# Attention probabilities turned by VectorE in 32x32 blocks instead of by TensorE, in the second batch of each middle group

## The chip, the cores and the metric

The kernel runs on one core of one Trainium2 chip. The metric is the device time of one launch in microseconds (us). The engines are named as in the profile: PE is TensorE (PEld its weight loads), DVE is VectorE, ACT is ScalarE, POOL is GpSimd, SP is SyncE, which here only issues DMAs.

## The reference, cut to what matters

Sixteen batches of 128 rows with 1024 features go through one layer: cross attention (32 query heads, 8 key and value heads, 32 features each) with a residual, and a feed-forward product with a residual, both after a layernorm.

```
B, S, EMBED, NUM_Q, NUM_KV, HEAD_DIM = 16, 128, 1024, 32, 8, 32
Q = layernorm(x) @ Wq + bq;  K = ctx @ Wk + bk;  V = ctx @ Wv + bv
scores = einsum('bhgqd,bhkd->bhgqk', Q, K) / sqrt(HEAD_DIM)
w = softmax(scores, axis=-1)
y = einsum('bhgqk,bhkd->bhgqd', w, V)
x = x + y @ Wo + bo
x = x + ffn_scale * (ei(layernorm(x)) @ ffn_kernel)      # ei: last 205 features scaled by -4
```

All is float32. On TensorE a float32 matmul is two passes, each with its own weight load, so the profile counts each matmul twice; the transposes by TensorE are one pass.

## The kernel before

The sixteen batches are taken in eight groups of two (GB = 2, T = 256 rows). While one group's attention runs, the PE works for its neighbours: the output projection of the group before (`out_proj`, names o_u, o_v, o_c), keys and values of the next (`prep_k`, `prep_v`), queries of the next (`prep_q`, names q_u, q_v, q_c), and the feed-forward products (`ffn`, name f). Groups 1 to 6 are the middle groups; the first and the last are run in their own way.

A small planner, the class `Stream`, writes all this out in one fixed order. It keeps a clock `now` by estimated PE time. `stream.add` queues work in pieces, each of which says how long it holds the PE; `stream.later(us, fn)` sets an event at a planned time; `stream.run(until)` fires events that are due and takes pieces in between. Each engine then executes its own instructions in that order, and waits where data or a buffer is not ready. There are no priorities at run time.

Attention of a group has four steps, one for each batch and half of the heads (`a` = 0 or 1, 16 query heads each), in the order batch 0, batch 1, batch 0, batch 1. In a step:

- `scores` (L568): 16 matmuls of 32 rows each; head group `i` of four uses the PE's row tile `i` and writes its own PSUM bank, tile `sc`. The four tiles come from the pool `ps_sc` with four buffers.
- For each `i`, at planned times 0.7 + 2.4 i: `exponentials` (L580 a row maximum by DVE, L584 four exponentials by ACT), and 2.3 us later `divide` (L595, L596, both DVE), which leaves the probabilities `p` with queries on the partitions.
- Half a step later, less 3 us, `turn` (L601): four transposes of 128x128 by PE into PSUM, and a copy to SBUF by ACT (L603), tile `pt`: now the keys are on the partitions.
- Near the end of the step `weighted` (L611): for each `i` one matmul of 32 columns by 512, four column tiles of the PE side by side, tile `av`; ACT copies the result to `yT` (L619), which `out_proj` reads in the next group.

The planned length of a step is `length` (23.2 us in most middle groups). The loop over steps:

```
pts = attend(b, a, length)
stream.run(start + length - 2.0)      # the last step: until the queue is empty
stream.run(stream.now, lambda: None in pts)
weighted(b, a, pts)
stream.now += 1.0
```

Weights of the projections come in pieces of 512 KB through a ring of eight buffers (`fetch`, L225), one for each that has been used; rows for the next groups, contexts and residuals are loaded from DRAM. All of these are issued by SP, in the planner's order. `through_dram` and `split_blocks` (L728) already use DVE's transposes of 32x32 blocks for the layernormed rows.

## Time and profile before

| what | value |
|---|---|
| time, three runs | median 788.25 us (787.9 to 791.28) |
| profiled execution | 788.44 us, of which the profiled span is 786.7 us |
| granted PE clock, mean | 0.997 |
| busy: PE, DVE, ACT, POOL | 767.2, 486.3, 322.4, 112.2 us |
| DMA | 192.42 MB, mean 245 GB/s; main queue 74.9% of 16 engines |

In the profile an instruction group reads: line, engine, operation, output<-input, size, number, then busy time and the mean of one in ns, then the idle time of the engine just before and what ended it. A duration of a matmul includes the pipeline behind it, so several overlap, and busy time of the PE is the union. A timeline row reads: start in us from the span's start, duration, engine, line, operation, count.

### The profile page before, as it was taken

Reading aid. Unit: us, or ns where it says so; the run is one execution under the profiler, and the core shown is the slowest. Engines: PE = TensorE matmul, PEld = TensorE weight load, DVE = VectorE, ACT = ScalarE, POOL = GpSimd, SP = SyncE. Lnnn points to the kernel's source line nnn. Section 1 sums busy time; section 2 is a strip of 40 time slices with the busy share of each in tenths; the row PEclk is TensorE's granted clock in tenths of the full one; section 3 lists DMA queues with packets and bytes.
Section 4 is the critical chain, followed back from the end, with each engine's and each line's share of the span. In section 5 each row is a group of like instructions: output and inputs, shape, how many; then the busy total and the mean of one; then the engine's idle time right before and its main releaser. Section 6 shows DMA issues by size and latency. Waiting matters only on the chain.

```text
span 786.7 us, 13740 instructions
## 1 busy us (share of the span) xinstructions
PE 767.2 (98%) x5008; PEld 571.6 (73%) x5008; DVE 486.3 (62%) x886; ACT 322.4 (41%) x1261; POOL 112.2 (14%) x142
## 2 busy tenths in 40 slices
PE   5998999999999999999999999999999999999997
PEld 4886884589746997479864898558984699556476
DVE  2158647756766567566774667856676666765552
ACT  0254764444334443344433444334434445575100
POOL 4154703020010102010020200202001010103000
PEclk9999999999999999999999999999999999999999
DMA  9999799988698776978778785987869657763802
GB/s 248 344 309 303 273 341 392 268 226 282 216 322 230 238 235 232 306 204 261 239 240 271 213 272 188 305 257 202 266 209 328 206 192 238 250 202 104 264 27 81
DMA packets 99268, 192.42 MB, mean 245 GB/s; under 512 B 8240, under 2 KB 57456, under 8 KB 99200
## 3 DMA queue, kind: packets, MB, share of 16 engines
q1 hardware_dynamic: 97568, 189.43, 74.9%
q0 software_dynamic: 528, 1.12, 0.6%
q10 hardware_dynamic: 1104, 0.98, 0.6%
q8 instruction: 40, 0.66, 0.3%
q14 instruction: 28, 0.23, 0.1%
HBM read 161.09 MB, written 30.41 MB: 243 GB/s over the span
## 4 chain that ended last, share of the span: by engine, by line
PE 88%; DVE 4%; DMA 2%; issue 2%; ACT 1%; POOL 1%; SPq 0%; POOLq 0%; DVEq 0%
PE f L323 14%; PE o_u L662 13%; PE q_u L451 12%; PE o_v L662 7%; PE tpp L601 7%; PE q_v L451 6%; PE k L323 6%; PE v L323 6%; PE sc L568 4%; PE av L611 4%; PE q L323 3%; PE o_c L662 3%; PE q_c L451 3%; DVE p L596 1%; DMA piece<-o 1%
## 5 line engine op out<-in xcount | busy, mean ns | idle before, releaser
L584 ACT ACTIVATE p<-sc,negm 128x128 f32<-128x128 f32 x512 | 181.1, 368 | 134.4 <-DVE negm L580 72.5
L603 ACT COPY pt<-tpp 128x512 f32<-128x512 f32 x128 | 74.6, 591 | 148.1 <-PE tpp L601 147.9
L580 DVE TENSOR_REDUCE negm<-sc 128x4 f32<-128x512 f32 x128 | 86.8, 680 | 59.3 <-PE sc L568 59.3
L584 ACT ACTIVATION_READ_ACCUMULATOR p<-sc,negm 128x1 f32 x512 | 105.5, 206 | 0.0
L323 PE MATMUL f<-wf_sb,x2l 128*128 128x512 f32 x256 | 104.3, 408 | 0.0
L323 PE MATMUL f<-wf_sb,x2h 128*128 128x512 f32 x256 | 100.5, 393 | 0.0
L596 DVE TENSOR_TENSOR p<-p,inv 128x512 f32<-128x512 f32 x128 | 90.9, 710 | 4.4
L451 PE MATMUL q_u<-t,piece 128*128 128x128 f32 x672 | 81.3, 275 | 0.0
L601 PEld LDWEIGHTS tpp<-ident,p 128*128 128x128 f32 x512 | 62.2, 141 | 24.9 <-issue 16.8
L601 PE MATMUL tpp<-ident,p 128*128 128x128 f32 x512 | 76.4, 274 | 3.7 <-DVE p L596 3.5
L451 PEld LDWEIGHTS q_u<-t,piece 128*128 128x128 f32 x672 | 78.0, 192 | 0.1
L180 POOL TENSOR_TENSOR x<-x,bo_b 128x256 f32<-128x256 f32 x64 | 53.6, 862 | 155.7 <-DMA x<-in_x_dram 155.7
L323 PE MATMUL v<-wv_sb,cT 128*128 128x256 f32 x256 | 62.2, 393 | 9.0 <-DMA wv_sb<-in_L_xattn_Wv_dram 7.1
L662 PE MATMUL o_v<-piece,s 128*128 128x512 f32 x128 | 60.3, 598 | 0.5 <-DVE x L676 0.5
L323 PEld LDWEIGHTS v<-wv_sb,cT 128*128 128x128 f32 x256 | 48.4, 197 | 15.8 <-DVE cT L349 9.4
L662 PE MATMUL o_u<-piece,s 128*128 128x512 f32 x128 | 59.2, 594 | 0.6 <-DVE x L676 0.6
L323 PE MATMUL k<-cT,wk_sb 128*128 128x256 f32 x256 | 58.3, 380 | 1.0 <-DVE cT L349 1.0
L662 PE MATMUL o_u<-piece,yT 128*128 128x512 f32 x128 | 58.6, 599 | 0.0
L323 PEld LDWEIGHTS f<-wf_sb,x2l 128*128 128x128 f32 x256 | 48.2, 188 | 10.6 <-issue 1.1
L323 PEld LDWEIGHTS k<-cT,wk_sb 128*128 128x128 f32 x256 | 47.9, 190 | 10.2 <-issue 2.6
L323 PEld LDWEIGHTS f<-wf_sb,x2h 128*128 128x128 f32 x256 | 48.2, 188 | 9.6 <-issue 0.5
L568 PEld LDWEIGHTS sc<-kT,qT 32*128 32x128 f32 x1024 | 31.4, 186 | 25.8 <-issue 25.8
(86 smaller groups left out, 935.1 us busy)
## 6 DMA issues: line engine op xcount, KB each, us to landing
piece<-o SPq DMA_DIRECT2D x64, 512.0 KB, 5.0
piece<-q SPq DMA_DIRECT2D x56, 512.0 KB, 5.1
piece<-in_L_xattn_Wq_dram SPq DMA_DIRECT2D x50, 512.0 KB, 5.2
piece<-in_L_xattn_Wo_dram SPq DMA_DIRECT2D x48, 512.0 KB, 4.6
xn<-in_x_dram SPq DMA_DIRECT2D x16, 512.0 KB, 6.8
x<-in_x_dram SPq DMA_DIRECT2D x16, 512.0 KB, 4.6
ctx<-in_ctx_dram SPq DMA_DIRECT2D x60, 128.0 KB, 6.6
out_dram<-x SPq DMA_DIRECT2D x15, 512.0 KB, 2.7
```

Of the source, the lines that this page charges most:

```text
L180: lambda cut=cut: nc.gpsimd.tensor_add(x_t[:, cut], x_t[:, cut], bo_b[:, cut]) and None,
L323: nc.tensor.matmul(mm, lhsT=lhsT, rhs=rhs, start=k == 0, stop=k == n - 1)
L451: nc.tensor.matmul(mm if part is None else mm[:, part], lhsT=lhsT, rhs=rhs, start=start and n == k == 0, stop=k == len(some) - 1, skip_gro ...
L568: nc.tensor.matmul(tiles[i][:, g], lhsT=qT[rows, g], rhs=kT[rows, a, cols], start=True, stop=True,)
L580: nc.vector.tensor_reduce(negm, tile_, AX.X, ALU.max, negate=True)
L584: nc.scalar.activation(p[:, g], tile_[:, g], AF.Exp, bias=negm[:, g : g + 1], accum_out=total[:, g : g + 1],)
L596: nc.vector.tensor_mul(p, p, inv.unsqueeze(2).to_broadcast([P, NG, S]))
L601: nc.tensor.transpose(tp[:, g], p[:, g], ident)
L603: nc.scalar.copy(pt, tp)
L611: nc.tensor.matmul(mm[i * HD : (i + 1) * HD], lhsT=vs[b][:, h * HD : (h + 1) * HD], rhs=pts[i], start=True, stop=True,)
L662: nc.tensor.matmul(mm, lhsT=lhsT[:, 2 * k + c], rhs=w[:, c], start=start and k == c == 0, stop=k == c == 1, skip_group_check=True,)
```

## The change

In the second batch of each middle group (`by_blocks`: batches 3, 5, 7, 9, 11, 13; 12 steps of the 32), the probabilities are no longer turned by PE.

- DVE transposes each 32x32 block of `p` in place (`turn_blocks`) after `divide`. Partition quarter `k` then holds the keys of every block `t`, for the queries of block `k`.
- `weighted_blocks` multiplies with the PE divided in 16 tiles of 32x32: for key block `t`, head group `i` and query block `k` one matmul of 32 keys by 32 features against 4 x 32 columns; the four `t` are summed in PSUM. Row tile `k` writes its own PSUM bank.
- Each quarter of the partitions needs all keys' values. So the values of such a batch are stored to DRAM, and loaded four times, once for each quarter (`load_values`), into half of the buffers `pt_all` that the other batch's turned probabilities use. This is done after each of the first batch's two sums, as these buffers are overwritten between.
- The four score tiles become one tile of four banks with one buffer, which `weighted_blocks` uses for its sums as well. Turned probabilities of the other steps go to one fixed buffer `pt_all` instead of a pool of four.
- The planned lengths are 22.4 for 23.2, and 18.6 for 19.2. The block sum stands at `length - 4.0` in its step.

```
-    ps_sc = ctx.enter_context(tc.tile_pool(name="ps_sc", bufs=4, space=PSUM))
+    ps_sc = ctx.enter_context(tc.tile_pool(name="ps_sc", bufs=1, space=PSUM))
...
             vs[b] = v
+            if by_blocks(b):
+                stream.later(2.0, lambda b=b, v=v: nc.sync.dma_start(out=v_dram[b], in_=v) and None)
...
-        tiles = [ps_sc.tile([P, NG, S], FP, tag="sc", name=f"sc_{b}_{a}_{i}") for i in range(NI)]
+        sc = ps_sc.tile([P, NI, NG, S], FP, tag="sc", name=f"sc_{b}_{a}")
...
+    NK = S // HD
+    pt_all = const.tile([P, NI, NG * S], FP, name="pt_all")
+    v_dram = [dram.tile([P, KV], FP, name=f"v_dram{b}") for b in range(B)]
...
-        pt = work.tile([P, NG, S], FP, tag="pt", name=f"pt_{b}_{a}_{i}", bufs=4)
-        nc.scalar.copy(pt, tp)
+        nc.scalar.copy(pt_all[:, i].rearrange("p (g s) -> p g s", g=NG), tp)
...
+    def by_blocks(b):
+        return GB <= b < B - GB and b % GB == 1
+
+    def repeated(b):
+        vr = pt_all[:, 2 * (b % GB) : 2 * (b % GB) + 2].rearrange("p i n -> p (i n)")
+        return vr.rearrange("p (t n) -> p t n", t=NK)
+
+    def load_values(b):
+        for k in range(NK):
+            nc.sync.dma_start(
+                out=repeated(b)[k * HD : (k + 1) * HD],
+                in_=v_dram[b].rearrange("(t r) n -> r t n", t=NK),
+            )
+
+    def turn_blocks(p):
+        blocks = p.rearrange("p g (t k) -> p g t k", t=NK)
+        nc.vector.transpose(blocks, blocks)
+
+    def weighted_blocks(b, a, pts):
+        av = ps_sc.tile([P, NK, NG, S], FP, tag="sc", name=f"av_{b}_{a}")
+        for t in range(NK):
+            for i in range(NI):
+                head = slice(i * HD, (i + 1) * HD)
+                for k in range(NK):
+                    rows = slice(k * HD, (k + 1) * HD)
+                    nc.tensor.matmul(
+                        av[head, k, :, :HD],
+                        lhsT=repeated(b)[rows, t, a * P + i * HD : a * P + (i + 1) * HD],
+                        rhs=pts[i][rows, :, t * HD : (t + 1) * HD],
+                        start=t == 0,
+                        stop=t == NK - 1,
+                    )
+        yTs[b, a] = work.tile(S4, FP, tag="yT", name=f"yT{b}_{a}", bufs=4)
+        nc.scalar.copy(
+            yTs[b, a].rearrange("p g (k q) -> p k g q", k=NK), av[:, :, :, :HD]
+        )
...
+                def by_vector():
+                    divide(b, a, i, p, total)
+                    turn_blocks(p)
+                    pts[i] = p
...
+                if by_blocks(b):
+                    stream.later(2.3, by_vector)
+                else:
+                    stream.later(2.3, lambda: divide(b, a, i, p, total))
+                    stream.later(length / 2 - 3.0, by_tensor)
...
-            length = 17.4 if first else 23.2 if grp < NGRP - 2 else 19.2
+            length = 17.4 if first else 22.4 if grp < NGRP - 2 else 18.6
...
+                if by_blocks(b):
+                    stream.run(start + length - 4.0)
+                    stream.run(stream.now, lambda: None in pts)
+                    weighted_blocks(b, a, pts)
+                    stream.now += 2.1
+                    if q == 2 * NA - 1:
+                        stream.run(start + length, lambda: stream.queue)
+                    else:
+                        stream.run(start + length)
+                    continue
...
                 weighted(b, a, pts)
                 stream.now += 1.0
+                if by_blocks(b + 1):
+                    load_values(b + 1)
```

More of the change, by code (lines that the diff above doesn't have):

```diff
@@ L568, in scores @@
                 nc.tensor.matmul(
-                    tiles[i][:, g],
-                    lhsT=qT[rows, g],
-                    rhs=kT[rows, a, cols],
-                    start=True,
-                    stop=True,
+                    sc[:, i, g], lhsT=qT[rows, g], rhs=kT[rows, a, cols], start=True, stop=True
                 )
-        return tiles
+        return sc
     def exponentials(b, a, i, tile_):
@@ L601, in turn @@
             nc.tensor.transpose(tp[:, g], p[:, g], ident)
-        pt = work.tile([P, NG, S], FP, tag="pt", name=f"pt_{b}_{a}_{i}", bufs=4)
-        nc.scalar.copy(pt, tp)
-        return pt
+        nc.scalar.copy(pt_all[:, i].rearrange("p (g s) -> p g s", g=NG), tp)
+        return True
     def weighted(b, a, pts):
@@ L613, in weighted @@
                 lhsT=vs[b][:, h * HD : (h + 1) * HD],
-                rhs=pts[i],
+                rhs=pt_all[:, i],
                 start=True,
@@ L755, in attend @@
     def attend(b, a, length):
-        tiles = scores(b, a)
+        sc = scores(b, a)
         stream.now += 1.2
@@ L763, in first, with by_tensor @@
             def first(i=i):
-                p, total = exponentials(b, a, i, tiles[i])
-                stream.later(2.3, lambda: divide(b, a, i, p, total))
-                def third():
+                p, total = exponentials(b, a, i, sc[:, i])
+                def by_vector():
+                    divide(b, a, i, p, total)
+                    turn_blocks(p)
+                    pts[i] = p
+                def by_tensor():
                     pts[i] = turn(b, a, i, p)
                     return 0.45
-                stream.later(length / 2 - 3.0, third)
+                if by_blocks(b):
[3 more added lines that the diff above has]
+                    stream.later(length / 2 - 3.0, by_tensor)
             stream.later(0.7 + 2.4 * i, first)
```

## The prediction

> **What bounds the kernel now.** I read the page's engine table first, then the chain that ended last, then the list of PE's waits.

> ```profile
> PE 767.2 (98%) x5008; PEld 571.6 (73%) x5008; DVE 486.3 (62%) x886; ACT 322.4 (41%) x1261; POOL 112.2 (14%) x142
> PE 88%; DVE 4%; DMA 2%; issue 2%; ACT 1%; POOL 1%; SPq 0%; POOLq 0%; DVEq 0%
> ```

> TensorE (PE) is busy 98% of the span and is 88% of the chain; the clock was granted whole (0.997). A microsecond taken from PE in a middle group is a microsecond of the run, as long as nothing else becomes late. PE's own waits in the list are 7.1 us on the first weights, 3.5 us on DVE's probabilities (all before 80 us), and under 2 us on anything else: nothing else is late now.

> Next, what the removed work costs. The groups:

> ```profile
> L601 PE MATMUL tpp<-ident,p 128*128 128x128 f32 x512 | 76.4, 274 | 3.7 <-DVE p L596 3.5
> L603 ACT COPY pt<-tpp 128x512 f32<-128x512 f32 x128 | 74.6, 591 | 148.1 <-PE tpp L601 147.9
> L596 DVE TENSOR_TENSOR p<-p,inv 128x512 f32<-128x512 f32 x128 | 90.9, 710 | 4.4
> L728 DVE STREAM_TRANSPOSE turn_f<-turn_f 128x512 f32<-128x512 f32 x28 | 19.7, 704 | 0.0
> ```

> Durations of matmuls overlap, so I priced by starts, in PE's timeline (start, us, count):

> ```profile
> 322.27 0.59 PE L662 MATMUL o_v<-piece,s 128*128 128x512 f32 x1
> 322.70 1.04 PE L601 MATMUL tpp<-ident,p 128*128 128x128 f32 x8
> 323.57 0.59 PE L662 MATMUL o_v<-piece,s 128*128 128x512 f32 x1
> ...
> 308.15 0.40 PE L323 MATMUL f<-wf_sb,x2h 128*128 128x512 f32 x1
> 308.48 1.07 PE L611 MATMUL av<-pt,v 128*32 128x512 f32 x8
> 309.48 1.17 PE L568 MATMUL sc<-kT,qT 32*128 32x128 f32 x32
> 310.58 0.70 PE L662 MATMUL o_u<-piece,yT 128*128 128x512 f32 x1
> ```

> Eight transposes push the stream back by 0.87 us: 0.109 each. The weighted sum (av) holds PE from 308.48 to 309.48: 1.00 us for four 32-column tiles, two passes each. The scores (sc) hold it for 1.10.

> Last, how small tiles run side by side: PE's windows of the scores alone, all from the start of the burst (busy, instructions so far):

> ```profile
> 309.47:309.68 0.21, 0.20 (x4) 1.00 0.91 371
> 309.47:309.79 0.32, 0.31 (x8) 1.00 0.94 384
> 309.47:309.90 0.43, 0.42 (x12) 1.00 0.98 400
> 309.47:310.60 1.13, 1.12 (x32) 1.00 0.96 388
> ```

> Four row tiles start together (0.007 us apart in the trace), then four more every 0.112 us; the first turn takes 0.213. Of 32 passes the last four start 0.903 after the first. All tiles that the shape allows work at once, here and in av.

> **The change part by part.** By the order of instructions it bears on 12 steps: the second batch of the six middle groups, two halves each.

> *Removed, per step.* 16 transposes by 0.109 = 1.75 us, and av 1.00: 2.75 us of PE, all on the path. ACT loses four copies of 0.59 (28 us in all): off the path, worth nothing.

> *Added on PE.* 64 matmuls of 32x32, 128 columns, two passes: 128 passes, eight for each of sixteen tiles. Borders: av stood directly before sc and shared one; the new burst stands alone, so it pays a switch out of 0.10 (o_u starts that long after sc's streams end) and 0.10 to load the next weights, beside the entry of 0.10 that av had as well. With Y for the burst and 0.1 for its end: Y + 0.30 against 2.75. Saved per step: 2.45 - Y.

> No row shows sixteen tiles. Lower bound of Y: sc's turns, eight by 0.112 = 0.90. Upper bound: only four at once as in both rows, 32 turns by 0.112 = 3.58. The rows agree in kind (every tile that exists runs), which puts Y near the lower end. But sixteen starts 0.007 apart fill a turn of 0.112 entirely, so any hiccup lengthens it. I take 1.2: saved 1.25 per step, 12 x 1.25 = 15.0 us.

> [...]

> *Added on DVE.* Four 32x32 transposes per step by 0.70 (L728's row) = 2.8 us, 34 us in all, 62% to 66%; queued behind them are the next reduction, the divisions and the reads of PE's accumulators. In ten steps it is covered: the burst comes 18.1 us after the step's scores (work of PE between, by the rows above), while the last division now ends 12.7 to 13.0 us after them; 2.8 more is 15.8. Without this cover each microsecond of lateness would cost ten. In the last middle group (19.2 us steps) the burst comes 13.8 and 14.3 us after the scores, and the divisions end at 12.8 and 14.2. There DVE is the late one:

> ```profile
> 663.39 0.69 DVE L732 TENSOR_TENSOR x2l<-turn_f,x2h 128x512 fp32r<-128x512 f32 x1 [0.34 <-ACT x2h L729]
> 664.00 0.17 DVE L595 RECIPROCAL inv<-total 128x4 f32<-128x4 f32 x1
> 664.21 0.69 DVE L596 TENSOR_TENSOR p<-p,inv 128x512 f32<-128x512 f32 x1
> ```

> That step began at 650.7, and DVE has under 1 us of idle before 664; the transposes end near 14.2 + 2.5 = 16.7, a wait of 2.4 us (none to 2.5). The other step has some 2 us idle: 0.6 (none to 1.5). I take 3 us together.

> *Added waits on PE.* The scores buffer now also holds the burst's sums, so the next scores wait for ACT's copy of them. Between stand 1.3 us of PE work in half of the steps, 2.3 or so in the others. Before, ACT's copy (0.58) ended 0.67 us after av: covered, cost nothing; without cover up to 0.7 x 12 = 8 us.

> *Added transfers.* Per batch, SP issues one store of the values (128 KB) and, after each of the first batch's two sums, four loads of 128 KB; the first load waits for PE's sum. Behind it on SP stand the weight pieces, rows and residuals. SP already waits for PE before nearly every piece (L225 <- PE, some 290 us), and eight pieces are ahead of PE, so a load more costs nothing. Loads of this kind land in 3.8 to 6.6 us, needed after 18. About 7 MB on 192: 75% busy becomes 78%. With the cover gone, PE would wait a landing, some 5 us, per step.

> *Planner.* Steps are planned at 22.4 and 18.6 instead of 23.2 and 19.2; this moves PE's work among steps and takes none away.

> Sum against the profiled execution's own 788.4 us (span 786.7; the median of the runs, 788.25, is the same within 0.2): 788.4 - 15.0 + 3.0 = 776.4. With 0.6 for small delays behind DVE's longer bursts: **777 us**.

> **Rivals.** *Four at a time* (slower): the sixteen tiles overlap only four deep. Y = 3.58, 12 x (2.45 - 3.58) = -13.6, plus 3: 805 us. For: no row shows more than four in flight. Against: four is all those shapes offer. It decides from Y = 2.2, below 6.5 tiles at once.
> *PE's sequencer feeds too slowly*: 256 instructions (load and matmul) in a burst. In the trace eight instructions stand between two semaphore events of PE's sequencer 0.074 us apart (at 48.2, 137.6, 598.7), at most 0.0092 each; about 33 wait in the queue at a burst's start. The other 223 would take 2.06 us: 12 x (2.45 - 2.06) = 4.7, less 3: 787. Against: two semaphore events with nothing between lie 0.055 to 0.060 apart, which leaves 0.002 per instruction.
> *DVE late in all steps*: 18.58 of 24.6 us are busy in the steps from 284.9; with 1 us of lateness in the ten covered steps as well, 787.

> **How the numbers follow.** Forecast (Y from 0.9 to 1.6) 0.56; slow feeding or a late DVE 0.19; four at a time 0.19, other slowdowns 0.06. About 0.5%, 4 us, is what the measurement can tell. The middle cases fall partly faster, mostly within 0.5%: faster 0.63, same 0.12, slower 0.25. Low end: Y = 0.9 and no late DVE, 788.4 - 18.6 = 770. High end: 796, halfway into the slower case, which leaves out less than 2 in 10. The forecast's own range is 770 to 782.

> **What would show it.** Right: PE's new row at L656 holds PE about 1.2 to 1.5 us per step from entry to exit, transposes fall from 512 to 320, groups of 93.8 us become about 91.3, and PE waits for DVE only at the two last bursts. Wrong: first and last of the 128 passes more than 2 us apart, a wait of the scores on ACT's copy, or of the burst on the value loads.

## The result and the profile after

The changed kernel takes 798.96 us (median of four runs, 795.51 to 802.11) against 788.08 us (787.23 to 791.28) for the kernel before on the same chip: 1.0123 times as long, 95% interval 1.0102 to 1.0145. It is slower, by 9.7 us in the ratio's terms, and the predicted 777 us and the range 770 to 796 both miss it. Measured again on another occasion (**again**, below) it took 1.0078 times as long [1.0056, 1.01], with single times from 791.5 to 803.0: it is slower each time, by a varying amount. The profiled execution took 796.58 us, span 794.8.

The engine table and the chain of the page after (busy us, share of the span, instructions; below it the shares of the chain):

```profile
PE 763.5 (96%) x6256; PEld 570.9 (72%) x6256; DVE 517.9 (65%) x934; ACT 296.8 (37%) x1213; POOL 112.9 (14%) x142
PE 75%; DVE 13%; ACT 4%; issue 4%; DMA 3%; POOL 1%; SPq 0%; POOLq 0%; DVEq 0%; ACTq 0%
```

PE is busy 3.7 us less than before, and yet the span is 8.1 us longer: PE now waits for others. Its share of the chain fell from 88% to 75%, DVE's rose from 4% to 13%, and "issue", time without a cause that the profile shows, from 2% to 4%. The list of PE's waits (what waits for what, us in total, times, longest) says where:

```profile
PE tpp L606 <- DVE p L594: 4.9, 3, 3.2
PE f L323 <- DVE x L793: 4.4, 5, 0.9
PE sc L570 <- issue: 2.8, 2, 2.5
...
PE sc L570 <- ACT p L582: 0.9, 1, 0.9
...
PE f L323 <- issue: 0.4, 1, 0.4
```

The first row was 3.5 before; the other four rows did not exist. The removed and the added work, in the groups and in the view of the new line:

```profile
L607 ACT COPY pt_all<-tpp 128x512 f32<-128x512 f32 x80 | 46.8, 592 | 68.8 <-PE tpp L606 64.3
L606 PE MATMUL tpp<-ident,p 128*128 128x128 f32 x320 | 47.8, 273 | 5.1 <-DVE p L594 4.9
```

```profile
L656 PE MATMUL av<-p,pt_all x1536: 264/268/295, 167.0 to 672.7; 32*32 32x128 f32 x192
```

192 transposes and 48 of ACT's copies are gone, and 1536 small passes have come (12 bursts of 128). PE's timeline shows what one burst holds:

```profile
217.97 0.39 PE L323 MATMUL f<-wf_sb,x2h 128*128 128x512 f32 x1
218.29 1.90 PE L656 MATMUL av<-p,pt_all 32*32 32x128 f32 x128
220.12 0.50 PE L323 MATMUL f<-wf_sb,x2l 128*128 128x512 f32 x1
```

From the f pass before to the one after it are 2.15 us, where two f passes otherwise stand 0.23 apart: a burst costs 1.92 us. Its first and last pass start 1.63 us apart, in all bursts but the last two.

**Where the 8.1 us of the span are.** The two traces are compared from one step's scores to the next (32 steps; the start of each is the first pass at the scores' line). This accounts for one execution, 796.58 us, and not for the median. What a burst step gains is taken from **combo_early** below, where nothing in the covered burst steps waits.

| part | us |
|---|---|
| until the first scores (43.73 after 41.13; 1.7 of it a half clock near 17 us) | +2.6 |
| steps 0 to 4 (waits of step 1 longer by 1.4; before, a half clock fell there) | +0.1 |
| PE's work in the 24 steps with and between bursts | -8.4 |
| f waits for DVE, five steps of 25.44 in place of 24.26 | +5.9 |
| PE without instructions: 4.5, 0.8 and 0.7, with the half clock that follows the first | +6.0 |
| last burst waits for DVE | +0.6 |
| last group: scores wait for ACT's `p` (0.9), transposes longer for DVE (0.3), 0.2 unexplained | +1.4 |
| sum (measured 8.1) | 8.2 |

The fourth row in DVE's timeline (in brackets the idle time before and what ended it):

```profile
212.13 0.71 DVE L645 STREAM_TRANSPOSE p<-p 128x512 f32<-128x512 f32 x1
212.77 1.24 DVE L283 BATCH_NORM_STATS2 st_a<-xn 128x6 f32<-128x512 f32 x2
...
215.17 0.81 DVE L292 TENSOR_SCALAR xq<-xn,mv_a,rs_a 128x1024 f32<-128x1024 f32 x1 [0.73 <-POOL rs_a L291]
215.90 0.75 DVE L793 SCALAR_TENSOR_TENSOR x<-f,fscale,x 128x512 f32<-128x512 f32 x1
```

The last transposed block ends at 212.8, well before the burst at 218.3. But the normalization of the next x stands behind it, with 0.73 us of waiting for POOL, and only then does DVE read f's sums (215.90). PE wanted that accumulator at 215.8 and got it at 216.7. In the kernel before, no row of f waits for DVE.

The fifth row in PE's timeline, and in the windows of the same stretch (us, then busy time of PE, PEld, DVE, ACT, POOL, the granted clock, DMA share and GB/s):

```profile
170.29 0.93 PE L570 MATMUL sc<-kT,qT 32*128 32x128 f32 x19
173.69 1.10 PE L570 MATMUL sc<-kT,qT 32*128 32x128 f32 x13 [2.47 <-issue]
```

```profile
172.00:174.00 2.00, 0.31 (x9) 0.31 (x10) 1.31 (x2) 0.00 (x0) 2.00 (x4) 0.97 0.03 6
174.00:176.00 2.00, 2.00 (x18) 1.78 (x15) 2.00 (x4) 0.27 (x2) 1.61 (x2) 0.50 0.59 173
```

In the middle of one burst of scores, whose operands are all there, PE stops for 2.47 us. After that its clock is granted at a half for 3.41 us, which loses another 1.7. The DMA queues tell what came meanwhile. In the stretch 167.0 to 171.2:

```profile
q1 hardware_dynamic: 527, 1.20, 100.1%
```

and in 171.2 to 172.3:

```profile
q1 hardware_dynamic: 28, 0.07, 18.4%
q8 instruction: 1, 0.02, 5.5%
```

Queue q8 carries PE's program, by its count: 49 packets of 0.80 MB in all, 16 KB each, for 12,512 matmuls and weight loads, one packet per 255 of them; before it were 40 packets (0.66 MB) for 10,016. The kernel's data kept the DMA engines full until 171.2; then came the one q8 packet, landing at 172.23, and PE went on 1.46 us later.

Now count PE's instructions in the trace: matmuls, weight loads and waits for semaphores. All three waits that end in "issue" stand at the same place of a block of 256, give or take one, and so do all twelve such waits in the further traces. So they are borders between two packets of the program. PE went on 1.46, 1.28 and 1.32 us after a q8 packet landed. There is one packet for each border: numbered in order, packet and border start within 5.5 us of each other for 47 of the 49 in this trace, and for 38 of the 40 before. In the fifteen waits the packet that PE waited for started about when PE's passes reached the border before (0.4 us ahead at the earliest) or up to 4.5 us later. Before, the shortest time from one border to the next was 11.7 us. Now a burst is 256 instructions by itself, and eight borders follow the one before within 7 us, the closest within 2.3 us not counting the wait itself.

### The profile page after: what moved, and what is told of

Read it like the earlier page. It is cut to its first block, busy times and chain, and to the rows that moved or that the text cites. A ratio compares the mean times of both kernels' runs of the same rounds, so it can differ in the third digit from the quotient of the medians.

```text
span 794.8 us, 16177 instructions
## 1 busy us (share of the span) xinstructions
PE 763.5 (96%) x6256; PEld 570.9 (72%) x6256; DVE 517.9 (65%) x934; ACT 296.8 (37%) x1213; POOL 112.9 (14%) x142
## 3 DMA queue, kind: packets, MB, share of 16 engines
q0 software_dynamic: 528, 1.12, 0.7%
## 4 chain that ended last, share of the span: by engine, by line
PE 75%; DVE 13%; ACT 4%; issue 4%; DMA 3%; POOL 1%; SPq 0%; POOLq 0%; DVEq 0%; ACTq 0%
PE o_u L709 12%; PE q_u L453 9%; PE f L323 7%; PE o_v L709 6%; PE v L323 6%; PE k L323 6%; PE q_v L453 5%; PE sc L570 4%; PE tpp L606 4%; PE q L323 3%; PE o_c L709 3%; DVE p L594 3%; PE av L656 3%; PE q_c L453 3%; ACT p L582 3%
## 5 line engine op out<-in xcount | busy, mean ns | idle before, releaser
L323 PE MATMUL f<-wf_sb,x2l 128*128 128x512 f32 x256 | 103.6, 405 | 4.4 <-DVE x L793 4.4
L323 PE MATMUL f<-wf_sb,x2h 128*128 128x512 f32 x256 | 100.5, 393 | 0.4 <-issue 0.4
L607 ACT COPY pt_all<-tpp 128x512 f32<-128x512 f32 x80 | 46.8, 592 | 68.8 <-PE tpp L606 64.3
L323 PE MATMUL v<-wv_sb,cT 128*128 128x256 f32 x256 | 62.2, 397 | 10.1 <-DMA wv_sb<-in_L_xattn_Wv_dram 8.1
L323 PEld LDWEIGHTS v<-wv_sb,cT 128*128 128x128 f32 x256 | 49.8, 199 | 18.8 <-DVE cT L349 9.6
L323 PEld LDWEIGHTS f<-wf_sb,x2l 128*128 128x128 f32 x256 | 48.1, 188 | 18.5 <-DVE x L793 6.6
L323 PE MATMUL k<-cT,wk_sb 128*128 128x256 f32 x256 | 57.2, 380 | 1.2 <-DVE cT L349 1.2
L323 PEld LDWEIGHTS k<-cT,wk_sb 128*128 128x128 f32 x256 | 48.4, 190 | 11.0 <-issue 3.1
L323 PEld LDWEIGHTS f<-wf_sb,x2h 128*128 128x128 f32 x256 | 48.2, 188 | 10.7 <-issue 1.2
L606 PEld LDWEIGHTS tpp<-ident,p 128*128 128x128 f32 x320 | 38.3, 141 | 23.3 <-issue 20.3
L606 PE MATMUL tpp<-ident,p 128*128 128x128 f32 x320 | 47.8, 273 | 5.1 <-DVE p L594 4.9
```

Source lines behind the costliest of these rows:

```text
L323: nc.tensor.matmul(mm, lhsT=lhsT, rhs=rhs, start=k == 0, stop=k == n - 1)
L606: nc.tensor.transpose(tp[:, g], p[:, g], ident)
L607: nc.scalar.copy(pt_all[:, i].rearrange("p (g s) -> p g s", g=NG), tp)
```

## The experiments

Each number is a median, with its ratio to the kernel before on the same chip. "Again" is the reference for edits of the changed kernel, and "under again" compares two medians; they come from several chips, on which the kernel before took 788.8 to 789.4 us.

**again**: the changed kernel, unchanged.

> The changed kernel once more, unchanged. Theory F (instruction supply): the 256 PE instructions of a block burst and the 64 of the scores after it use up a 16 KB chunk of PE's instructions in some 4 us, and the next chunk, fetched by DMA only when PE's sequencer enters the one before it, can come later than that. PE then idles with releaser issue, only where a chunk ends. Those idle times come again, 2 to 7 us in all, but in other steps or of other sizes, as the fetch waits for whatever stands before it in the DMA queues; the five waits of f for DVE, 0.88 us each, come again in the same places. Rival S (the start): the 2.6 us that the first scores come later than in the kernel before (43.7 for 41.1) is caused by the new buffers, and comes again; if it is chance, it differs. Time 795 to 802 us.

Measured: 795.83 us (791.51 to 802.96, twelve runs), ratio 1.0078 [1.0056, 1.01]. In its trace the five waits of f for DVE are there again (0.87 to 0.88 each), as is the 0.87 of the scores for ACT; of waits ending in issue there is one, 0.74, where 2 to 7 us had been expected. So the DVE waits belong to the program's order and are a constant loss, while the missing instructions differ from one execution to the next. That they make the spread of the times is likely, but not shown: see combo.

**one_block**: 16 of the 64 matmuls of a burst.

```
-        for t in range(NK):
+        for t in range(1):
...
-                        stop=t == NK - 1,
+                        stop=True,
```

> Only the first of the four key blocks is summed: 16 matmuls in a burst instead of 64, so 48 of 64 products are left out; all else stays. Theory P (PE work alone): the burst falls from 1.63 us between first and last pass to about 0.25, 12 x 1.4 = 17 us less: 779 to 784 us. Theory F adds that with 64 PE instructions in a burst no chunk is used up in 4 us: no idle time with releaser issue in or near the bursts, another 3 to 6 us less: 774 to 779.

Measured: 777.64 us (776.77 to 778.48), ratio 0.9853 [0.9837, 0.9868], 18.2 us under again, which is in the range of theory F. In the traces a burst step where nothing waits is 1.4 us shorter (21.34 in place of 22.74), 16.8 us in twelve. So the burst is paid by PE. No wait ends in issue here, 256 instructions never take less than 10.2 us, and the times lie within 1.7 us.

**no_turns**: DVE's block transposes left out, so that the bursts multiply by unturned probabilities.

```
                     divide(b, a, i, p, total)
-                    turn_blocks(p)
```

> The DVE transposes of the probabilities are left out, so the products are taken of unturned blocks; all else stays. Theory D (DVE late): the five waits of f for DVE (0.88 us each) and the wait of the last burst go, 4 to 6 us less: 790 to 796 us. Theory F alone: DVE has no part in it, the idle times with releaser issue stay, 795 to 802.

Measured: 792.31 us (788.82 to 797.08), ratio 1.0035 [1.0018, 1.0052], 3.5 under again. Of the five waits of f for DVE three are gone, 0.83 and 0.41 are left; a wait of 2.75 ends in issue. DVE's 34 us of transposes cost 3.5. The bursts' own waiting is the small part of it: the steps of the last two bursts are 0.2 and 0.6 shorter. The five steps of f are still 2.5 us longer than in rows_later, in place of 5.9, so the transposes are not all that makes f wait; what else does (the shorter planned steps, say) was not tested.

**buffers_only**: no bursts, the lengths of before; what stays are the one score tile and `pt_all`.

```
     def by_blocks(b):
-        return GB <= b < B - GB and b % GB == 1
+        return False
```

> The changed kernel with block sums in no step and the old planned lengths: what is left of the change is one score tile of four banks instead of four tiles, and one fixed buffer for the turned probabilities instead of a pool of four. Theories F, D and P: no burst, no transposes, so 788 us as before, no idle time with releaser issue. Rival B (buffers): the scores or copies wait for the shared buffers, or the start comes 2.6 us later: 790 to 793 us.

Measured: 793.27 us (792.29 to 793.56), ratio 1.0046 [1.0034, 1.0058]. The prediction had the buffers at nothing; they cost 3 to 4 us. In the waits of its PE is a row that the kernel before does not have, and the transposes wait 4.9 us for DVE in place of 3.5:

```profile
PE sc L570 <- ACT p L582: 0.9, 1, 0.9
```

The middle groups are as long as before. The loss is in the first group and the last, whose steps are shorter: the next scores write the one tile, and can't start before all four head groups of the last ones are exponentiated.

**pt_only**: the kernel before with only `pt_all`.

```
-        pt = work.tile([P, NG, S], FP, tag="pt", name=f"pt_{b}_{a}_{i}", bufs=4)
-        nc.scalar.copy(pt, tp)
-        return pt
+        nc.scalar.copy(pt_all[:, i].rearrange("p (g s) -> p g s", g=NG), tp)
+        return True
```

> The kernel before, with only the turned probabilities in one fixed tile pt_all (four score tiles as before, no burst, lengths as before). Theory that the one score tile is what the buffers cost: as before, 788 to 789. Rival, that pt_all costs it (the copies into it wait for the weighted sums of the step before, in the first group above all): 792 to 793 as buffers_only. If it is shared: about 790 to 791.

Measured: 789.68 us (787.87 to 789.96), ratio 1.0006 [0.9992, 1.0019]: nothing measurable. The transposes wait 3.5 us for DVE, as before. So the single score tile is what costs.

**four_tiles**: the changed kernel with four one-bank score tiles again, the burst's sums in four such tiles, four copies by ACT.

```
-        av = ps_sc.tile([P, NK, NG, S], FP, tag="sc", name=f"av_{b}_{a}")
+        av = [ps_sc.tile([P, NG, S], FP, tag="sc", name=f"av_{b}_{a}_{k}") for k in range(NK)]
...
+        for k in range(NK):
+            nc.scalar.copy(yTs[b, a][:, :, k * HD : (k + 1) * HD], av[k][:, :, :HD])
```

> The changed kernel, with a tile of its own for each head's scores again (four of one bank in place of one of four banks), and the burst's sums in four such tiles, which ScalarE copies one by one (four copies in place of one); pt_all stays. Theory that the one score tile is what the buffers cost: the 3.9 us of buffers_only go (the 0.87 us wait of the scores for ScalarE near 697, and the longer waits of the first group), so about 3 to 4 us faster than again (795.8): 792. Rival, that pt_all is what costs: same as again, 796, and the four copies add up to 12 x 0.2 us if they hold the next scores.

Measured: 791.01 us (788.33 to 792.58), ratio 1.0022 [1.0004, 1.004], 4.8 under again. The scores' wait for ACT is gone (step 29 shorter by 0.7), as is the last burst's (0.6), and the transposes' wait for DVE is back at 3.5 us. The five waits of f remain, as does one of 0.94 that ends in issue.

**rows_later**: the changed kernel, the normalizations of x 1.5 us later.

```
-                stream.later((10.0 if grp == 2 else 5.0) + 4.0 * j, lambda b=b: rows_x(b))
+                stream.later((10.0 if grp == 2 else 6.5) + 4.0 * j, lambda b=b: rows_x(b))
```

> The changed kernel, with the two normalizations of x after each group's last burst due 1.5 us later, so that VectorE reads f's sums before it waits for GpSimd. Theory that f's sums are read late behind the normalization that the transposes pushed back: the five waits of f for VectorE (0.87 us each, 4.4 us) go, and the time is 4 us under again (795.8): 792. Rival, that the time comes back at once elsewhere (the normalized x is late for its way through DRAM, or VectorE reads the next sums late): three or more waits of 0.5 us or longer at other places, and 795 to 796.

Measured: 791.86 us (784.4 to 794.92), ratio 1.0028 [0.9997, 1.006], 4.0 under again. All five waits of f are gone (steps of 24.26 in place of 25.44), and no new wait for DVE over 0.4 us has come. But the trace has waits ending in issue of 2.46 and 1.00 us; the fastest run, 784.4, is the only one of the six with a mean clock of 1.000.

**split_burst**: each burst in two halves, 4 us apart.

```
+                    stream.run(start + length - 7.6)
+                    stream.run(stream.now, lambda: None in pts)
+                    weighted_blocks(b, a, pts, 0)
+                    stream.now += 1.05
+                    stream.run(start + length - 3.5)
+                    weighted_blocks(b, a, pts, 1)
```

> The changed kernel, with each burst in two halves (products 0 and 1 of each sum about 4 us earlier, 2 and 3 about where the burst was): the same instructions, spread out. Theory that PE runs out of instructions where 256 of them go by in 1.6 us and the next 16 KB of its program has not come: no idle time of PE that ends in issue of more than 0.3 us, the spread of the single times within 4 us (again had 11), and 1 to 4 us under again (795.8): 792 to 795; against it 12 x 0.1 to 0.2 us more for the second start of the sixteen tiles. Rival, that these idle times come from something else (a queue, chance of the run): idle times ending in issue of 1 us or more remain, and the times spread over 8 us or more.

Measured: 795.9 us (794.18 to 798.25), ratio 1.0091 [1.0073, 1.0108]. No wait ends in issue any more, and the spread is 4.1 us, as the theory had it (five runs only, against again's twelve); 256 instructions now take 5.3 us at least. The median misses: in the last middle group the earlier half waits for DVE (1.70) and then for ACT and DVE (1.71 and 1.20, with the half clock after them), 7.8 us in these two steps that the expectation had not counted.

**combo**: four_tiles and rows_later together.

> The changed kernel with the edits of four_tiles and rows_later together: four one-bank score tiles again, and the normalizations of x 1.5 us later. Theory, step by step from the traces: against again (795.8) the five waits of f go (1.17 us in each of five steps, 5.8 us) and the buffers' waits of the first and last groups (0.7 + 0.6 + 0.3 + 1.3, about 3 us): 787 us, with PE still running out of instructions in some runs (spread of 6 us or more), and 782 to 783 where it does not. Rival, that the two edits share their gain: 790 to 791 as each alone.

Measured: 789.24 us (787.96 to 790.86), ratio 1.0002 [0.9993, 1.0011]. Neither expectation: better than each alone, 2 us above the theory's 787. What the two edits took away came back as missing instructions: three waits ending in issue, 3.0 us together. Yet the eleven times lie within 2.9 us, where the theory had 6 or more; so such waits do not by themselves make the times spread. One of the three:

```profile
219.19 1.15 PE L570 MATMUL sc<-kT,qT 32*128 32x128 f32 x26
221.56 0.50 PE L570 MATMUL sc<-kT,qT 32*128 32x128 f32 x6 [1.21 <-issue]
```

This one comes with the edit. The later normalization moves the stores of the normalized x (`dram_x`, 512 KB each). SP issues two of them in combo, and then in again, at (start, duration of both issues):

```profile
214.41 4.75 SPq L314 DMA_DIRECT2D dram_x<-xq  x2
```

```profile
215.56 1.77 SPq L314 DMA_DIRECT2D dram_x<-xq  x2
```

In combo the first store is 0.9 us ahead of the border before (215.31), and the packet of program starts 4.0 us after that border. In again the store is 1.0 us behind the border (214.58), and the packet starts 0.97 after it. Eight traces have the whole burst at this place. In the five with the normalization at its old time (after, again, four_tiles, no_turns, no_values) the store is behind the border and the packet starts 0.5 to 1.0 us after it; in the three with the later one (rows_later, combo, combo_no_values) the store is ahead and the packet starts 3.6 to 4.0 us after. Only these three wait there, by 1.0 to 1.2 us. So here a packet of program comes late when data has been issued just ahead of it.

**combo_early**: combo, with the bursts of the first five middle groups 3.5 us earlier in their steps.

```
-                    stream.run(start + length - 4.0)
+                    stream.run(start + length - (7.5 if grp < NGRP - 2 else 4.0))
...
-                stream.later((10.0 if grp == 2 else 6.5) + 4.0 * j, lambda b=b: rows_x(b))
+                stream.later((10.0 if grp == 2 else 8.0) + 4.0 * j, lambda b=b: rows_x(b))
```

> As combo, with each burst of the first five middle groups 3.5 us earlier in its step, so that four-row products and f's long ones lie between it and the next scores (and the normalizations of x 3 us later than in the changed kernel, so that they stay behind f's sums). Theory that PE runs out of instructions where a burst and the scores after it go through one chunk of 256: idle time of PE ending in issue falls to under 0.5 us, the times spread over 5 us at most, and the median is 1 to 4 us under combo's: 783 to 786. Rival, that the spread comes from elsewhere: the same median and spread as combo. Other rival: a burst that begins 3.5 us earlier waits for VectorE's last transposed block (the slack is 4.5 us): one or more waits of av for p in steps other than the last two.

Measured: 782.03 us (780.95 to 783.8), ratio 0.9909 [0.9895, 0.9922]: 7.2 us under combo and as much under the kernel before. It beats both kernels. The chain of the profiled execution (span 779.2, PE busy 97%):

```profile
PE 89%; DVE 3%; DMA 3%; issue 2%; ACT 1%; POOL 1%; SPq 0%; POOLq 0%; DVEq 0%
```

The chain is PE's again, and in the list of waits there is none of f or of the bursts for DVE, and none that ends in issue (the last burst but one has passes that come 0.24 us late, too short for the list). Close borders are still there, though: the closest pair is 2.6 us apart, and **columns_first** below shows what that can do. From the first burst's group to the end of the middle groups it takes 541.2 us against 549.7 before: 8.4 us, or 0.70 per burst. That is what the change is worth where it is made.

**no_values** and **combo_no_values**: again and combo without the values' store and loads (the bursts multiply by what `pt_all` holds).

```
-            if by_blocks(b):
-                stream.later(2.0, lambda b=b, v=v: nc.sync.dma_start(out=v_dram[b], in_=v) and None)
...
-                if by_blocks(b + 1):
-                    load_values(b + 1)
```

> The changed kernel without the store of the values and without their loads in four copies (the bursts multiply by what pt_all holds). The prediction had these 7 MB at nothing. Theory that they are covered: as again, 795 to 796, with the idle times that end in issue still there. Rival, that they hold something up (the queue of the loads, or the fetch of PE's program behind them): 2 us or more under again, and no idle time of over 1 us that ends in issue.

> As combo, without the store of the values and their loads in four copies (the bursts multiply by what pt_all holds). no_values was 3.6 us under again by medians, with intervals that touch. Theory that these transfers delay the fetches of PE's program: 786 to 787 against combo's 789.2, idle times ending in issue of 1.5 us or less in the trace (combo 3.0). Rival, that they are covered and no_values was chance: 788.5 to 790.

Measured: 792.18 us (791.27 to 796.84), ratio 1.0046 [1.0025, 1.0068], and 784.42 us (782.58 to 787.9), ratio 0.9954 [0.9934, 0.9974]. The first interval still touches again's, the second is clear of combo's: in combo the 7 MB cost 4.8 us by the medians, 3.8 by the ratios. Each trace has one wait ending in issue, of 0.95 and 1.06 us, as the rival of the first and the theory of the second had it; the second time is lower than its theory's 786. No row of PE's waits names these transfers. In the two combos' traces the largest difference is step 6, after the first burst: 25.76 against 22.35, a wait ending in issue of 1.31 and a half clock against none. (Another 1.3 us in step 1 is a half clock near 80 us that only combo's trace has; it comes and goes among the traces.) In the 5 us before that place the queues were, in combo:

```profile
q1 hardware_dynamic: 612, 1.31, 92.8%
```

and in combo_no_values:

```profile
q1 hardware_dynamic: 276, 0.94, 55.2%
```

The packet starts 3.2 us after the border before in combo and 1.2 in combo_no_values. This fits a packet of program that has to pass through engines kept full by data, but it is one place in one pair of traces. At the borders near 215 and 494 the packets come about as late with the values as without; there it is the store of x that stands ahead of them, as told under combo. So the time is shown, and the way it is lost only made likely.

**half_columns** and **columns_first**: combo_early with half of each burst's columns (half of the query heads left out), and with the two inner loops of the burst exchanged.

```
-                        rhs=pts[i][rows, :, t * HD : (t + 1) * HD],
+                        rhs=pts[i][rows, : NG // 2, t * HD : (t + 1) * HD],
```

```
-            for i in range(NI):
...
-                for k in range(NK):
+            for k in range(NK):
...
+                for i in range(NI):
```

> As combo_early, but each matmul of a burst streams 64 columns in place of 128 (half of the query heads are left out, and ScalarE copies the half that is there twice): the same number of instructions, half the streaming. In the changed kernel the first 32 of a burst's 128 passes start 0.007 us apart, then there is a gap of 0.109, then they start 0.017 apart. Theory that PE's sequencer feeds the burst (some 32 passes waiting at its start, the rest as they come, two instructions each): first to last pass 1.5 to 1.65 us, as with 128 columns (1.63). Rival, that the streams of the sixteen tiles set it: 0.8 to 1.1 us. Looked at in the trace only.

> As combo_early, with the two inner loops of a burst exchanged (successive matmuls go to another column tile of the same row tile, in place of another row tile of the same column tile). Theory that PE's sequencer feeds the burst: 1.55 to 1.7 us from the first to the last pass, as before (1.63). Rival, that tiles which share rows or columns hold each other up: other than 1.63 by 0.2 us or more, either way. Looked at in the trace only.

Measured: from the first to the last pass 1.26 us, and 1.63 us. (One run each: 780.5 and 782.78 us.) In what order the tiles are taken makes no difference. Half the streaming shortens the burst by 0.38 only, which is neither expectation. If the streams' part goes with the columns, it is an estimated 0.4 of the 1.26 us at 64 columns and 0.75 of the 1.63 at 128; the rest is something else. The first 32 passes start within 0.3 us in all three kernels, 0.007 apart; then they come 0.017 apart for a while. That looks like a queue that is full at the start and is then refilled at that pace, but it was not isolated.

columns_first has combo_early's schedule, and its trace holds what combo_early's does not:

```profile
351.04 1.24 PE L323 MATMUL v<-wv_sb,cT 128*128 128x256 f32 x5 [1.09 <-issue]
```

This is a border 3.2 us behind the one before, in products of the values just after a burst. In combo_early the same two borders are 2.6 us apart, but the packet started 0.4 us before PE's passes reached the first of them, and here 1.8 us after. So moving the bursts away from the scores makes these waits rare; it does not rule them out.

**before_again**: a second trace of the kernel before.

> The kernel before, for a second trace of it. The first scores began at 41.1 us in the first trace and at 41.4 to 44.0 us in those of its variants. Theory that this start is chance (when the first weights and ctx land): another value than 41.1 by 0.5 us or more, the steps after it the same to 0.05 us. Rival, that the kernel before always starts at 41.1 and the single score tile costs the start 1.4 us or more: 41.0 to 41.3.

Measured: 787.67 us, first scores at 41.30 us, the steps from 2 on within 0.25 us of the first trace and nearly all within 0.04. So the start did not move here; 41.30 lies at the edge of the rival's range, and the expected 0.5 us did not show. Over all traces the first scores began at 41.1 to 42.7 us with four score tiles (nine traces) and at 42.1 to 44.6 with one (eight). The traces tell where the difference lies. From the seventeenth PE pass to the first scores it is 26.63 us in twelve of the seventeen traces, with either kind of tile. It is 0.4 and 0.5 more in two (no_values, split_burst), and 1.7 more in the three that have a half clock near 17 us (after, one_block, rows_later). The rest is in the first sixteen passes, which wait for the first weights and contexts: the seventeenth starts at 14.5 us in the first trace of the kernel before, and at 14.7 to 16.6 in the others. The program is the same up to there; that the tile has no part in these landings is argued and not shown.

## Why the prediction was wrong, step by step

The change does save time where it is made, 8.4 us in place of 15.0. It came out slower because of terms that the sum had at nothing or did not have: readers queued behind the transposes, the single score tile, and the fetch of PE's program. Of the three signs of being wrong that were named none came up, except that the last burst, which waited for DVE, had 2.2 us from its first pass to its last.

- **Removed on PE, 2.75 us per step.** Right in kind: 512 transposes became 320, and av's 1.00 is gone. Four transposes cost 0.436 us beside the projections, but 0.36 between f's passes (0.59 from pass to pass in place of 0.23).
- **Y, the burst, 1.2 us.** Failed: 1.63 in ten bursts. The borders were right (0.29 for 0.30). With 1.63 in its place the sum gives 12 x (2.45 - 1.63) = 9.8 us instead of 15.0, and 8.4 were measured. Of the 48 groups of four transposes that are gone, 20 stood between f's passes; at 0.07 less each they make up an estimated 1.4 us, which is the difference. I had put Y near the lower bound because every tile that a shape offers was seen at work in bursts of 32 passes; those fit into the part that starts 0.007 us apart, and 128 don't. The rival of a slow supply had the direction and overpriced it (2.06); that a slow supply is the cause was not isolated. The ends 0.90 and 3.58 did hold the value.
- **DVE covered in ten steps, 3 us in the last two.** The bursts wait as told: none in ten steps, with 4.5 and 5.4 us of slack, and together under 1 us in the last two, for 3 predicted. (The rows read for it had one slip: of the 3.5 us of waits for DVE's probabilities before, 0.42 stands at 721.9 and not before 80.) What failed is the sentence before it, that the reads of PE's accumulators are queued behind the transposes: I named them and did not price them. In the last step of five of the six middle groups they cost 1.2 us, 5.9 in all (rows_later; no_turns takes away 3.4 of it).
- **The buffers, nothing but ACT's copy.** The copy is covered, as predicted; no wait of the scores for it appears. But a single tile also ties the next scores to the last head group's exponentials, and in the short steps of the first and the last group that shows: 3 to 4 us (buffers_only, four_tiles, and pt_only, which acquits `pt_all`).
- **The value transfers, nothing.** Failed in combo: 4.8 us by the medians. The 5 us of a late landing never came up, as PE does not wait for the values; the transfers seem to press on something that the prediction did not have at all.
- **Not in the sum: PE's program has to be fetched.** The rival of the slow sequencer counted how fast instructions leave the queue and not how they get there. At 256 instructions in 1.6 us, the next 16 KB were needed sooner than they landed: the packet of 171.27 landed 5.1 us after PE's passes had reached the border before. It cost 6 us in the profiled run, with the half clock that follows. No such wait stands in the one trace each of split_burst and combo_early, where the bursts are split or moved away from the scores; one of 1.09 stands in that of columns_first. Whether it also makes the times spread over 11 us stays open, as combo has such waits and a spread of 2.9.
- **The planner's lengths**, taken as no cost, were not tried by themselves, and may have a part in f's waits.

The sum with the sizes that were measured: 788.4 - 8.4 (work) + 5.9 (f) + 6.0 (program) + 0.6 + 1.4 (last burst, last group) + 2.7 (start and first group) = 796.6, the time of the profiled execution. The 2.7 of the start is mostly the first landings and a half clock, as told under before_again, so it reads as chance and not as a term.

## What to carry to other kernels

Where work is replaced by many short instructions, count them against the rate at which the program itself arrives (here a packet per 255 instructions, with 256 gone by in 1.6 us): keep a dense burst away from other dense work (combo_early, 7.2 us under combo), and don't fill the DMA engines just then (combo_no_values, 4.8 us under combo, by a way that was only made likely). When a queue gets longer, it is not its last consumer alone that must be checked but each reader behind it, with the time at which its buffer is wanted next (f's reads, 5.9 us). And merging buffers is free only in steps as long as those that one has looked at; look at the shortest (buffers_only, 3 to 4 us).
